# Graph network kernel: layer 1's passes in another order, degrees turned by a bf16 product of depth one, x's first loads moved up

## The chip, the cores and the metric

The kernel runs on one core of a Trainium2 chip. The metric is the device time of one launch in microseconds (us). The kernel before takes 2695.79 us (median of 3 runs, 2694.9 to 2703.81).

## The reference

Two SAGE layers, a linear layer, a residual and a layer norm, on 12,500 nodes with 256 features and 200,000 edges. The edges are sorted by `dst`, and low nodes have many more edges than high ones (`dst` is drawn as 12500 times the square of a uniform number).

```python
def sage(h, src, dst, W_l, b, W_r):
    agg = segment_sum(h[src], dst, N)              # sum over a node's edges
    deg = segment_sum(ones, dst, N)
    return (agg / maximum(deg, 1)[:, None]) @ W_l + b + h @ W_r

h = relu(sage(x, src, dst, W1_l, b1, W1_r))
h = relu(sage(h, src, dst, W2_l, b2, W2_r))
out = layernorm(x + h @ W3 + b3)
```

## The kernel before

The function `by_runs` does the work; `by_sorting` stands behind a flag for data that does not fit, and does not run here. Nodes and edges are cut into blocks and tiles of 128: 98 blocks of nodes, 1563 tiles of edges. The sums over edges are made in two ways.

**Low nodes, by counting.** The first 2,560 nodes have so many edges that a table of counts is made for them: how many edges go from each source node to each of these nodes. There are five groups (0 to 4) of 512 nodes (`COUNTED`). `count(g, to)` fills the table of group g tile by tile: DVE makes a pick and some zeros and ones (L719, L709, L725), TensorE (PE) makes two small bf16 products (L744, L746) in a bank `count_ps` of PSUM, of which there are three, and ACT casts the bank into the table (L754). The first 128 tiles, all of group 0, are added by DVE instead (L752). There are four buffers for tables; `HELD` says which group has which. A **pass** over group g (`passed`, `products`) then multiplies the whole of x by that table: for each pair of source blocks, SP loads 512 KB `rows<-x_d` (L584; three buffers, so two pairs ahead), DVE opens the packed counts (L567, L569), ACT widens them (L659, L661), and PE makes eight products of 512 columns (L682) that add up in the banks `dense_ps` and `beside_ps`. Four ACT copies (L690) end the pass.

**High nodes, by gathering.** A **round** takes four edge tiles: POOL issues four indirect DMAs of rows (`got`, L313), PE multiplies them by zeros and ones (`part_ps`, the strips, L339), ACT copies the result (L349), PE multiplies it again (`sum_ps`, L356, and L363 for the degree), and DVE adds it into a ring of sums (L369) and into a row of degrees, `degs`, which is partition 0 of the tile `spare` (L365). Layer 1 has 217 rounds.

**Blocks.** When a block's sums are complete, `first_block` finishes it in three pieces: it loads its own part x·W_r from `xw_d` (L992); it adds the bias on DVE (L1014); it turns the degrees from a row into a column, on PE by a transpose of `spare` in f32 (L1003), and DVE takes their reciprocal (L1007, L1008); `sage` multiplies the sums by W_l (L967), and h is stored. If the block's sums are known when the second piece starts, the transpose is made there, in the first third of a round, just behind the strips; the products L967 follow in the next third. Once in eight blocks, `overlap` first adds the ring's end to its beginning (DVE, L951 and L954).

**The order.** PE and POOL run in the order in which the program is written; the framework orders DVE, ACT and SP. `layer()` writes that order by a plan: it issues a round in three thirds and fills each third with pieces of dense work, until the planned load of one engine reaches a third, two thirds and all of `room_for`, which is 5.3 in layer 1. Costs such as `COST_PRODUCT` or `count_cost` are fixed numbers. When 8 rounds are left, `emptied()` writes all remaining dense work at once, and the last rounds follow without any.

Layer 1's stages (`stages_1`) are: splitting x, x·W_r and counting group 3; pass 3 with a third of the counting of groups 2, 1 and 0 (and the move of table 3 to DRAM); pass 2 with the second third; pass 1 with the rest; pass 0 with the counting of group 4; pass 4 alone. So the five passes hold 195, 190, 195, 92 and 0 counted tiles. Layer 2 makes five passes without counting.

**The start.** Edge lists and weights are loaded on SP's and ACT's queues, then DVE and PE make the tables for the first gathers, and `splitting()` loads x (`raw`, L609) and starts to multiply it.

Of the kernel before, what the change touches and what calls it, by code (L numbers as in the profile page):

```python
# [27 lines left out]
P = 128  # L28
# [23 lines left out]
def by_runs(  # L52
# [41 lines left out]
    RB = 8  # L94
# [121 lines left out]
    degs = spare[0:1]  # L216
# [167 lines left out]
    HELD = [counts[3], counts[2], counts[1], counts[0], counts[0]]  # L384
# [4 lines left out]
    near = counts_flat[1].bitcast(F32)[:, NP * CW // 2:].rearrange("p (b d) -> p b d", b=NP)[:, :, CW // 2 - NEAR:]  # L389
# [201 lines left out]

    def splitting():

        bufs = 5
        order = [*range(HOT1 // P, NB, 2), *range(0, HOT1 // P, 2)]
        assert NB % 2 == 0 and (HOT1 // P) % 2 == 0
        raw = {}

        def fetched(i):
            u = order[i]  # L600
            t = raw_pool.tile([P, 2, 2, D], F32, name="raw", bufs=bufs)
            whole = min(2, (N - u * P) // P)
            loads = []
            if whole < 2:
                left = N - (u + whole) * P
                nc.vector.memset(t[:, whole, 1], 0.0)
                loads.append(nc.sync.dma_start(t[:left, whole, 1], x[(u + whole) * P:N]))
            if whole:
                loads.append(nc.sync.dma_start(t[:, :whole, 1], x[u * P:(u + whole) * P].rearrange(  # L609
                    "(b p) d -> p b d", p=P)))  # L610
            return t

        def multiplied(i, v, x_t):
# [8 lines left out]
            b, s, pre = order[i], raw.pop(i), raw_pool.tile([P, 2, D], F32, name="pre", bufs=2)  # L622
# [10 lines left out]
        for i in range(len(order)):  # L633
            for k in range(i, min(i + bufs - 2, len(order))):
                if k not in raw:
                    raw[k] = fetched(k)
# [128 lines left out]
    def degrees(blocks):  # L765

        ps = beside_pool.tile([P, DN], F32, name="beside_ps")
        for b in range(blocks):
            n0 = b * P
            chunks = [c for c in range(HC) if at_most((c + 1) * P) + WIDEST > n0 and at_least(c * P) <= n0 + P]  # L770
            for c in chunks:
# [3 lines left out]
                for k in range(WIDEST):  # L775
                    nc.tensor.matmul(ps[:, b:b + 1], lhsT=begins[:, WIDEST - k:WIDEST - k + P],
                                     rhs=hist[:, c, k:k + 1], start=c == chunks[0] and k == 0,
                                     stop=c == chunks[-1] and k == WIDEST - 1)
# [97 lines left out]
    def stages_1(waiting):  # L876
# [13 lines left out]
        assert highs[2] - lows[2] < steps_of and highs[1] - lows[1] < steps_of  # L890
# [3 lines left out]
        yield [passed(waiting, 1, x2_d, into), (counted, cost)]  # L894
        yield [passed(waiting, 0, x2_d, into), counting(4)]
        yield [passed(waiting, 4, x2_d, into)]

    def stages_2(waiting):

        into = sums_a, sums_b  # L900
        HELD[3] = HELD[0]
# [4 lines left out]
    def all_found():  # L906

        sums_of = work.tile([P, FIELDS], F32, name="sums_of", bufs=1)
# [54 lines left out]
    def sage(b, agg, since, wl, own):  # L963

        ps = block_bank()
        for c in range(NC):
# [6 lines left out]
        given.add(b)  # L973
        nc.vector.scalar_tensor_tensor(own, ps[:, 0], rdeg[:, b:b + 1], own, op0=OP.mult, op1=OP.add)  # L974
# [14 lines left out]
    def first_block(b, agg=None):  # L989
# [7 lines left out]
        def summed(ps):  # L997
            nonlocal agg, deg_row, since
# [3 lines left out]
            r = (b % RB) * P  # L1002
            settled(nc.tensor.transpose(ps[:, NC], spare[:, r:r + P], ident), since)  # L1003

        def degree(ps):
            deg = work.tile([P, 1], F32, name="deg")
            nc.vector.tensor_scalar(deg, ps[:, NC, 0:1], 1.0, None, op0=OP.max)  # L1007
            nc.vector.reciprocal(rdeg[:, b:b + 1], deg)  # L1008

        known = of_ring and b in upto  # L1010
        if known:
            ps = turned()
# [831 lines left out]
```

## Time and profile before

| | |
|---|---|
| median of 3 runs | 2695.79 us |
| the profiled execution | 2719.84 us |
| its span, first to last instruction | 2717.6 us |
| granted PE clock, mean | 0.931 |
| split of x and x·W_r ends, pass 3 begins | about 340 us |
| end of passes 3, 2, 1, 0, 4 of layer 1 | about 546, 745, 965, 1180, 1367 us |
| layer 2's first pass begins | about 1419 us |
| layer 2's last pass ends | about 2586 us |
| HBM read, written | 541.82 MB, 93.15 MB |

The ends of the passes are the starts of the ACT copies L690. A row of the views reads: line, engine, operation, out<-in, shape, xcount, then busy time in us and the mean of one in ns, then the engine's idle time just before these instructions and what ended it. PE's products overlap one another, so that the busy time of a group is more than what the group adds to the time; the distance from one start to the next says more.

### The profile page before, as it was taken

What the parts mean: (1) busy time and instruction counts of PE and PEld (TensorE: products, weight loads), DVE (VectorE), ACT (ScalarE), POOL (GpSimd) and SP (SyncE); (2) the same over time, 40 slices, a digit from 0 to 9 for tenths busy, and PEclk for the clock granted to TensorE, in tenths of its full rate; (3) what the DMA queues carried; (4) which work ended last, traced back from release to release, by engine and by line L of the source; (5) the groups of instructions that cost most, each with busy time, mean ns of one, the idle gap of its engine ahead of it and who ended that gap; (6) DMA issues with size and microseconds to landing.
All of it is one profiled execution on the core that took longest, in us unless ns stands there. A gap on an engine that the chain in (4) does not pass through costs nothing.

```text
span 2717.6 us, 44003 instructions
## 1 busy us (share of the span) xinstructions
PE 2227.7 (82%) x13283; PEld 1535.7 (57%) x13283; DVE 1336.3 (49%) x4777; ACT 1198.1 (44%) x3325; POOL 1696.2 (62%) x1736
## 2 busy tenths in 40 slices
PE   5777788878888889878868888888888888888867
PEld 3545555555556656655635555566555655556545
DVE  5666466666667665544341233234334434444445
ACT  2434366654456655544424444443443344334312
POOL 5667566656666656666545666666666666666663
PEclk9889799999999989999978999999999999999988
DMA  8789877778787777878867877777776777667643
GB/s 225 260 267 308 283 230 230 234 231 253 253 263 238 238 240 246 267 257 272 272 196 264 273 239 232 245 233 218 245 233 208 219 230 220 197 202 226 205 138 102
DMA packets 282080, 638.07 MB, mean 235 GB/s; under 512 B 50913, under 2 KB 138795, under 8 KB 281835
## 3 DMA queue, kind: packets, MB, share of 16 engines
q1 hardware_dynamic: 193569, 407.49, 46.1%
q0 software_dynamic: 82848, 226.34, 27.1%
q8 instruction: 111, 1.82, 0.3%
q10 hardware_dynamic: 5418, 1.32, 0.3%
q14 instruction: 134, 1.10, 0.1%
HBM read 541.82 MB, written 93.15 MB: 234 GB/s over the span
## 4 chain that ended last, share of the span: by engine, by line
PE 40%; issue 6%; another core or an unknown queue 3%; DVE 2%; DMA 2%; ACT 2%; POOL 1%; SPq 0%; DVEq 0%; ACTq 0%; POOLq 0%
PE beside_ps L682 10%; PE dense_ps L682 9%; PE part_ps L339 5%; PE block_ps L967 4%; PE block_ps L1058 4%; PE sum_ps L356 3%; PE block_ps L1042 3%; PE block_ps L938 2%; POOL got L313 1%; DMA rows<-x_d 1%; ACT wide L661 1%; ACT some L349 0%; DVE sums L369 0%; DMA rows<-h_d 0%
## 5 line engine op out<-in xcount | busy, mean ns | idle before, releaser
L313 POOL DMA_INDIRECT got<-in_x_dram,src_t x863 | 871.9, 1010 | 514.1 <-issue 209.9
L313 POOL DMA_INDIRECT got<-h_d,src_t x851 | 811.3, 953 | 452.1 <-issue 225.9
L682 PE MATMUL dense_ps<-wide,rows 128*128 128x512 f32 x1960 | 885.7, 452 | 60.7 <-issue 23.6
L682 PE MATMUL beside_ps<-wide,rows 128*128 128x512 f32 x1960 | 798.0, 407 | 11.2 <-issue 7.2
L682 PEld LDWEIGHTS dense_ps<-wide,rows 128*128 128x128 f32 x1960 | 389.8, 199 | 190.0 <-issue 90.9
L661 ACT ACTIVATE wide<-spare 128x512 fp32r<-128x512 uint8 x490 | 306.7, 627 | 427.2 <-PE beside_ps L682 151.2
L682 PEld LDWEIGHTS beside_ps<-wide,rows 128*128 128x128 f32 x1960 | 388.8, 198 | 74.4 <-issue 18.6
L659 ACT CAST wide<-open 128x512 fp32r<-128x512 uint8 x490 | 300.4, 619 | 225.8 <-PE count_ps L746 72.7
L339 PE MATMUL part_ps<-got,one 128*32 128x257 f32 (+1 forms) x3472 | 299.6, 417 | 90.1 <-ACT some L349 46.5
L719 DVE TENSOR_SCALAR pick<-steps,tables,unit_t 128x175 bf16<-128x175 f16 (+3 forms) x784 | 250.5, 343 | 131.4 <-PE count_ps L746 68.8
L754 ACT CAST counts<-count_ps 128x225 f32 (+3 forms) x656 | 231.6, 353 | 160.2 <-PE count_ps L746 77.3
L369 DVE TENSOR_TENSOR sums<-sums,sum_ps 128x256 f32 x320 | 131.5, 411 | 287.1 <-PE beside_ps L682 98.5
L349 ACT COPY some<-part_ps 128x257 f32<-128x257 f32 (+1 forms) x320 | 118.1, 369 | 275.0 <-remote 67.7
L356 PEld LDWEIGHTS sum_ps<-two,some 128*128 128x128 f32 x1280 | 196.9, 200 | 46.9 <-issue 16.1
L356 PE MATMUL sum_ps<-two,some 128*128 128x128 f32 x1280 | 209.9, 287 | 16.2 <-issue 10.0
L263 DVE TENSOR_TENSOR one<-lo_t,lane_b 128x128 f32<-128x128 bf16 x430 | 122.6, 285 | 180.5 <-PE beside_ps L682 42.6
L339 PEld LDWEIGHTS part_ps<-got,one 128*32 128x32 f32 x3472 | 71.3, 111 | 240.9 <-issue 142.1
L746 PE MATMUL count_ps<-pick,low 128*128 128x175 bf16 (+3 forms) x784 | 176.6, 254 | 30.7 <-issue 15.3
L744 PE MATMUL count_ps<-aft,low 128*128 128x25 bf16 x652 | 117.3, 194 | 57.4 <-ACT counts L754 25.9
L618 PE MATMUL dense_ps<-w1r_sb,own_t 128*128 128x256 f32 x392 | 119.8, 433 | 46.2 <-issue 21.7
L746 PEld LDWEIGHTS <-low 128*128 128x128 bf16 x784 | 89.0, 120 | 99.0 <-issue 82.7
L974 DVE SCALAR_TENSOR_TENSOR own<-block_ps,rdeg,own 128x256 f32<-128x256 f32 x196 | 93.8, 478 | 98.5 <-PE sum_ps L356 17.0
(231 smaller groups left out, 2674.6 us busy)
## 6 DMA issues: line engine op xcount, KB each, us to landing
rows<-x_d SPq DMA_DIRECT2D x245, 512.0 KB
rows<-h_d SPq DMA_DIRECT2D x245, 512.0 KB
x_d<-raw SPq DMA_DIRECT2D x49, 512.0 KB
h_d<-split SPq DMA_DIRECT2D x98, 256.0 KB
got<-in_x_dram,src_t POOLq DMA_INDIRECT x863
got<-h_d,src_t POOLq DMA_INDIRECT x851
xw_d<-pre SPq DMA_DIRECT2D x49, 256.0 KB
own<-xw_d SPq DMA_DIRECT2D x98, 128.0 KB
```

The costliest lines, as they stand in the source:

```text
L263: nc.vector.tensor_tensor(one, lo[:, a:a + n * (G - 1) + 1:n].unsqueeze(2).to_broadcast([P, G, W]), lane_b[:, :W].unsqueeze(1).to_broadcas ...
L313: rows = nc.gpsimd.indirect_dma_start(out=g[:, j, X0:], out_offset=None, in_=table, in_offset=bass.IndirectOffsetOnAxis(ap=index[:, e:e + ...
L339: strip = nc.tensor.matmul(part_ps[j * W:(j + 1) * W, :width], lhsT=one[:, j], rhs=g[:, row, DW - width:], start=r == 0, stop=r == n - 1)
L356: nc.tensor.matmul(sum_ps[:, c], lhsT=some[:, x0 + c * P:x0 + (c + 1) * P], rhs=two, start=True, stop=True)
L369: adds.append(nc.vector.tensor_add(own, own, sum_ps[:, :NC]).ins)
L618: nc.tensor.matmul(ps[:, v * D:(v + 1) * D], lhsT=x_t[:, c], rhs=w1r_sb[:, c], start=c == 0, stop=c == NC - 1)
L659: nc.scalar.copy(wide.bitcast(F32R), counted)
L661: nc.scalar.activation(wide.bitcast(F32R), counted, AF.Copy, accum_out=seen[:, b % FIELDS, b // FIELDS:b // FIELDS + 1])
L682: nc.tensor.matmul(ps[c], lhsT=own, rhs=wide[u].bitcast(F32R), start=u + k == 0, stop=u == NB - 1 and k == 1)
L719: nc.vector.tensor_scalar(r[:, :w * NP], steps[:, :w * NP], key_t[g][:, t - lo_g:t - lo_g + 1], unit_t[:, t:t + 1], op0=OP.is_equal, op1=O ...
L746: nc.tensor.matmul(ps[:, :w * NP], lhsT=s, rhs=r[:, :w * NP], start=j == 0 and alone, stop=j == n_in - 1, skip_group_check=not alone)
L754: copies.append(nc.scalar.copy(to[:, :, bass.ds(off_act.at(t), w)], of).ins)
```

## The change

1. The passes of layer 1 run in the order 3, 2, 1, 4, 0. The counting of groups 2, 1, 4 and 0 is cut into four equal parts, one beside each of the passes 3, 2, 1 and 4; pass 0 runs alone at the end. The five passes now hold 169, 169, 157, 175 and 0 counted tiles. The buffers for the tables change places (`HELD`, `near`), and `room_for` goes from 5.3 to 5.2.
2. `degs` holds bf16. The transpose is replaced by a product of depth one: the row of 128 degrees is the weights, a single 1.0 the moving operand, and the column lands in the second half of the bank that `sage` already uses. It stands in `sage`, right ahead of the products with W_l, whether the block's sums are known earlier or not. A test that a degree is under 255.5 joins the tests on the data, and those are now added up in `all_found()` at the end of layer 2.
3. `degrees()` makes 221 products of one column instead of 260.
4. `w1r` and the first three loads of x are written ahead of the small loads and of the second copy of `dst` (`nxt_i`).

```diff
-    degs = spare[0:1]
+    degs = spare.bitcast(BF16)[0:1, :RN + P]
...
-    HELD = [counts[3], counts[2], counts[1], counts[0], counts[0]]
+    HELD = [counts[0], counts[2], counts[1], counts[0], counts[3]]
...
-                for k in range(WIDEST):
+                n_k = max(ROOMS[c * P // 32:(c + 1) * P // 32])
+                for k in range(n_k):
...
-        counted = chain(*(count(g, HELD[g]) for g in (2, 1, 0)))
-        cost = sum(counting(g)[1] for g in (2, 1, 0)) / 3
-        steps_of = sum(highs[g] - lows[g] for g in (2, 1, 0)) // 3
+        later_groups = 2, 1, 4, 0
+        counted = chain(*(count(g, HELD[g]) for g in later_groups))
+        cost = sum(counting(g)[1] for g in later_groups) / 4
+        tiles = [highs[g] - lows[g] for g in later_groups]
+        steps_of = sum(tiles) // 4
...
-        yield [passed(waiting, 1, x2_d, into), (counted, cost)]
-        yield [passed(waiting, 0, x2_d, into), counting(4)]
-        yield [passed(waiting, 4, x2_d, into)]
+        yield [passed(waiting, 1, x2_d, into), (islice(counted, steps_of), cost)]
+        yield [passed(waiting, 4, x2_d, into), (counted, cost)]
+        yield [passed(waiting, 0, x2_d, into)]
...
-    def sage(b, agg, since, wl, own):
+    def sage(b, agg, since, wl, own, deg_row=None):
         ps = block_bank()
+        if deg_row is not None:
+            product = nc.tensor.matmul(ps[:, 1, 0:1], lhsT=deg_row, rhs=lane_b[0:1, 1:2], start=True, stop=True)
+            settled(product, since)
...
+        if deg_row is not None:
+            deg = work.tile([P, 1], F32, name="deg")
+            nc.vector.tensor_scalar(deg, ps[:, 1, 0:1], 1.0, None, op0=OP.max)
+            nc.vector.reciprocal(rdeg[:, b:b + 1], deg)
...
-            settled(nc.tensor.transpose(ps[:, NC], spare[:, r:r + P], ident), since)
...
-        known = of_ring and b in upto
-        if known:
-            ps = turned()
-            summed(ps)
         nc.vector.tensor_add(own, own, biases[:, 0])
         yield 0.22, 0.4, 0.0
-        if of_ring and not known:
-            ps = turned()
-            summed(ps)
         if of_ring:
-            degree(ps)
-        h = sage(b, agg, since, w1l_sb, own)
+            overlap(b, True)
+            agg, deg_row = ring(b)
+            since = upto[b]
+        h = sage(b, agg, since, w1l_sb, own, deg_row)
...
+    w1r_sb = weight(w1r, "w1r_sb", "wr", nc.sync)
+    for i in range(3):
+        raw[i] = fetched(i)
...
-    nc.scalar.copy(spare, zero.to_broadcast([P, RN + P]))
+    nc.scalar.copy(degs, zero[0:1].to_broadcast([1, RN + P]))
...
-        layer(gathers_1, first_block, 3, staged(stages_1), 5.3, 8)
+        layer(gathers_1, first_block, 3, staged(stages_1), 5.2, 8)
```

The numbers of instructions hardly change. On PE, 78 transposes become 78 products of one column, and 39 of the products in `degrees()` go. All else is moved.

The first place is PE's order in one round of layer 1, from the strips (L339) of a round to a block's products with W_l; `dense_ps` and `beside_ps` are a pass's products. Before:

```order
L339 MATMUL part_ps<-got_99,one 32x257 x4
L1003 MATMUL block_ps<-ident,spare 128x128
L682 MATMUL dense_ps<-wide,rows 128x512
L682 MATMUL beside_ps<-wide,rows 128x512
L682 MATMUL dense_ps<-wide,rows 128x512
L682 MATMUL beside_ps<-wide,rows 128x512
L967 MATMUL block_ps<-w1l_sb,sums 128x256 x2
```

And after, from the strips of another such round:

```order
L339 MATMUL part_ps<-got_98,one 32x257 x4
L680 MATMUL dense_ps<-wide,rows 128x512
L680 MATMUL beside_ps<-wide,rows 128x512
L680 MATMUL dense_ps<-wide,rows 128x512
L680 MATMUL beside_ps<-wide,rows 128x512
L974 LDWEIGHTS spare
L974 MATMUL block_ps<-lane_b,spare 128x1
L977 MATMUL block_ps<-w1l_sb,sums 128x256 x2
```

The turn of the degrees has moved from behind the strips to the products with W_l; four products of the pass now lie ahead of it.

The second place is SP's queue at the end of layer 1's last pass: `rows<-x_d` are the pass's loads, `own` a block's part, `h_d` the stores of finished blocks. Before:

```order
L584 DMA rows<-x_d 128x1024 x3
L1027 DMA h_d<-own 128x256
L1030 DMA h_d<-split 128x512
L584 DMA rows<-x_d 128x1024
L992 DMA own<-xw_d 128x256
L584 DMA rows<-x_d 128x1024 x2
L1027 DMA h_d<-own 128x256
L1030 DMA h_d<-split 128x512
L584 DMA rows<-x_d 128x1024
L992 DMA own<-xw_d 128x256
```

And after:

```order
L584 DMA rows<-x_d 128x1024 x2
L1023 DMA h_d<-own 128x256
L1026 DMA h_d<-split 128x512
L584 DMA rows<-x_d 128x1024 x3
L1006 DMA own<-xw_d 128x256
L584 DMA rows<-x_d 128x1024 x7
```

With the smaller `room_for`, less of the last pass fits between the rounds, and the rest is written in one piece: 104 products of the pass follow one another on PE without anything between (before 32), and SP's last ten loads of rows have one other DMA among them.

The third place is SP's queue at the start, from its last load of a piece of `dst`; `counts1_120<-in_dst_dram` is `nxt_i`. Before:

```order
L1115 DMA counts0_119<-in_dst_dram 1x64
L1102 DMA counts1_120<-in_dst_dram 128x12x128
L1111 DMA counts1_120<-in_dst_dram 26x128
L1115 DMA counts1_120<-in_dst_dram 1x63
L1155 DMA w1r_sb_160<-in_L0_gnn_W1_r_dram 128x2x256
L609 DMA raw_254<-in_x_dram 128x2x256
L609 DMA raw_256<-in_x_dram 128x2x256
```

And after:

```order
L1111 DMA counts0_119<-in_dst_dram 1x64
L1126 DMA w1r_sb_146<-in_L0_gnn_W1_r_dram 128x2x256
L606 DMA raw_148<-in_x_dram 128x2x256
L606 DMA raw_150<-in_x_dram 128x2x256
L606 DMA raw_152<-in_x_dram 128x2x256
L1098 DMA counts1_120<-in_dst_dram 128x12x128
```

W1_r and three loads of x have passed the 768 KB of `nxt_i`.

More of the change, by code (lines that the diff above doesn't have):

```diff
@@ L590, in by_runs, with fetched @@
     AHEAD_OF = set()
-    def splitting():
[L594 to L611, printed above, removed]
+    X_BUFS = 5
+    x_order = [*range(HOT1 // P, NB, 2), *range(0, HOT1 // P, 2)]
+    assert NB % 2 == 0 and (HOT1 // P) % 2 == 0
+    raw = {}
+    def fetched(i):
+        u = x_order[i]
+        t = raw_pool.tile([P, 2, 2, D], F32, name="raw", bufs=X_BUFS)
+        whole = min(2, (N - u * P) // P)
+        if whole < 2:
+            left = N - (u + whole) * P
+            nc.vector.memset(t[:, whole, 1], 0.0)
+            nc.sync.dma_start(t[:left, whole, 1], x[(u + whole) * P:N])
+        if whole:
+            nc.sync.dma_start(t[:, :whole, 1], x[u * P:(u + whole) * P].rearrange("(b p) d -> p b d", p=P))
+        return t
+    def splitting():
         def multiplied(i, v, x_t):
@@ L621, in multiplied @@
                 return COST_AHEAD
-            b, s, pre = order[i], raw.pop(i), raw_pool.tile([P, 2, D], F32, name="pre", bufs=2)
+            b, s, pre = x_order[i], raw.pop(i), raw_pool.tile([P, 2, D], F32, name="pre", bufs=2)
             nc.scalar.copy(pre, ps.rearrange("p (b d) -> p b d", b=2))
@@ L632, in splitting @@
         ps, last = None, None
-        for i in range(len(order)):
-            for k in range(i, min(i + bufs - 2, len(order))):
+        for i in range(len(x_order)):
+            for k in range(i, min(i + X_BUFS - 2, len(x_order))):
                 if k not in raw:
@@ L906, in all_found @@
     def all_found():
+        many = work.tile([P, NB], F32, name="many", tag="x_sb")
+        nc.vector.tensor_scalar(many[:, HOT1 // P:], rdeg[:, HOT1 // P:], 1.0 / 255.5, 0.0, op0=OP.is_le, op1=OP.add,
+                                accum_out=test())
+        bad_ps = block_bank()
+        nc.tensor.matmul(bad_ps[0:1, 0, :TESTS], lhsT=ones, rhs=bad, start=True, stop=True)
+        n_unfit = work.tile([1, 1], F32, name="n_unfit", bufs=1)
+        nc.vector.tensor_reduce(n_unfit, bad_ps[0:1, 0, :TESTS], axis=mybir.AxisListType.X, op=OP.add)
         sums_of = work.tile([P, FIELDS], F32, name="sums_of", bufs=1)
@@ L995, in first_block @@
         yield 0.0, 0.0, 0.0
-        def summed(ps):
-            nonlocal agg, deg_row, since
+        nc.vector.tensor_add(own, own, biases[:, 0])
+        yield 0.22, 0.4, 0.0
+        if of_ring:
             overlap(b, True)
@@ L1147, in by_runs @@
             "(g j l) -> j g l", j=G, l=2 * P)[:, :, 0])
+    nxt_i = edges(dst, 1, later_on, "nxt_i", FAR, nc.sync)
+    last_edges(nxt_i, dst, 1)
+    with nc.allow_non_contiguous_dma(reason="one edge of each tile"):
         nc.scalar.dma_start(f1_i, dst[None, 0:HC * P * P:P])
         nc.scalar.dma_start(fours_i, dst[0:P * P:P * G][:, None, None].to_broadcast([P // G, G, 1]))
-    loads = []
-    def weight(w, name, tag, queue=nc.scalar):
-        t = consts.tile([P, NC, w.shape[1]], F32, name=name, tag=tag)
-        loads.append(queue.dma_start(t, w.rearrange("(c p) f -> p c f", p=P)))
-        return t
-    w1r_sb, w1l_sb = weight(w1r, "w1r_sb", "wr", nc.sync), weight(w1l, "w1l_sb", "wl")
+    w1l_sb = weight(w1l, "w1l_sb", "wl")
     biases = consts.tile([P, 2, D], F32, name="biases")
```

26 lines of the change are left out of this document (8 added, 18 removed).

## The prediction, made before the changed kernel ran

> **What bounds the kernel now.** I read the page's busy times first, then the busy time of each engine by stage, then the idle time just before groups of instructions.
>
> ```profile
> span 2717.6 us, 44003 instructions
> PE 2227.7 (82%) x13283; PEld 1535.7 (57%) x13283; DVE 1336.3 (49%) x4777; ACT 1198.1 (44%) x3325; POOL 1696.2 (62%) x1736
> ```
>
> PE is the busiest by far. The next view has one row for each pass of layer 1 (order 3, 2, 1, 0, 4): length, busy time of PE, PEld, DVE, ACT and POOL, granted clock, DMA share and GB/s.
>
> ```profile
> 340.00:546.00 206.00, 173.78 (x1184) 114.68 (x1183) 130.69 (x542) 129.41 (x344) 130.00 (x130) 0.96 0.74 230
> 546.00:745.00 199.00, 171.57 (x1048) 112.89 (x1047) 130.87 (x516) 98.94 (x233) 123.49 (x122) 0.95 0.78 246
> 745.00:965.00 220.00, 189.96 (x1322) 132.75 (x1321) 151.38 (x625) 130.94 (x375) 144.97 (x143) 0.98 0.78 246
> 965.00:1180.00 215.00, 181.86 (x1122) 124.74 (x1121) 123.00 (x469) 116.12 (x291) 137.35 (x140) 0.93 0.79 253
> 1180.00:1367.00 187.00, 159.10 (x849) 111.94 (x849) 74.64 (x262) 83.89 (x179) 106.93 (x112) 0.93 0.80 262
> ```
>
> PE idles 32, 27, 30, 33 and 28 us in the five passes: 14 to 16% in each, whether DVE is busy for 151 us of 220 or for 75 of 187. So PE's work and the small waits between its pieces set the time, and time is won by less PE work or fewer PE waits. Layer 2's passes take the rest, from 1419 us on; its PE order is the same row for row, so I count it at nothing.
>
> **Part 1: the degrees' turn.** L1003 is the transpose, L776 a bf16 product of one column, the nearest thing to the new product.
>
> ```profile
> L1003 PE MATMUL block_ps<-ident,spare 128*128 128x128 f32 x78 | 26.4, 339 | 18.6 <-DVE spare L954 11.5 <-issue 4.0 <-DVE sums L369 3.2
> L776 PE MATMUL beside_ps<-hist,begins 128*128 128x1 bf16 x260 | 10.1, 166 | 8.4 <-DVE begins L773 6.8 <-issue 1.1 <-DVE sums L369 0.4
> L776 PEld LDWEIGHTS <-begins 128*128 128x128 bf16 x260 | 9.4, 103 | 12.0 <-DVE begins L773 8.1 <-issue 1.6 <-DVE open L567 0.8
> L967 PEld LDWEIGHTS block_ps<-w1l_sb,sums 128*128 128x128 f32 x392 | 75.8, 200 | 21.5 <-issue 8.0 <-DVE open L567 0.5 <-DVE deg L1007 0.4
> 1333.03 0.33 PE L1003 MATMUL block_ps<-ident,spare 128*128 128x128 f32 x1
> 1333.12 0.48 PE L682 MATMUL dense_ps<-wide,rows 128*128 128x512 f32 x1
> ```
>
> A transpose lasts 339 ns but keeps the next product back by 0.09 us only (1333.03 to 1333.12). A product of one column adds 10.1/260 = 0.04 us. So at least 78 × (0.09 − 0.04) = 4 us go; by the means, 78 × (0.339 − 0.166) = 13.5 us. The other end: the new product is too short to cover the load of the sums behind it, and if those 200 ns stood open each time, it would cost 78 × (0.20 + 0.04 − 0.09) = 12 us more than before. 260 loads of weights of 103 ns were busy for 9.4 us together, so such loads run beside one another, and I stay with a gain. The row is nearer to 4 than to 13.5: I take **7 us less**.
>
> [...]
>
> Then the 18.6 us that PE waits ahead of the turn. The longest wait:
>
> ```profile
> 1219.76 0.61 PE L356 MATMUL sum_ps<-two,some 128*128 128x128 f32 x4
> 1227.86 0.47 PE L1003 MATMUL block_ps<-ident,spare 128*128 128x128 f32 x1 [5.89 <-DVE spare L954]
> 1226.40 0.28 DVE L365 TENSOR_TENSOR spare<-spare,sum_ps 1x128 f32 x1 [2.35 <-remote]
> 1227.53 0.27 DVE L954 TENSOR_TENSOR spare<-spare 1x128 f32<-1x128 f32 x1
> 1227.80:1233.00 5.20, 5.14 (x13) 4.11 (x14) 1.80 (x8) 2.17 (x6) 2.84 (x3) 0.50 0.64 217
> ```
>
> The turn is put down to DVE's L954. But DVE began L365, which needs products that PE shows at 1219.76, only at 1226.40, and it was free before: something else held everybody. Such a wait goes to whatever stands there next. So I leave the 11.5 us of L954 as they are. The other 7.1 (`issue` and `sums L369`) come from the turn standing right behind the strips; the new product stands four products of the pass later. I take **5 us less**, between 0 and 18.6.
>
> After that wait PE ran at a granted clock of 0.50 for 5 us. [...]
>
> DVE's maximum and reciprocal now wait for the new product, but L974 behind them waits for the products with W_l anyway. ACT's and DVE's operations on the degrees keep their counts and lengths (1x128). All this I cost at nothing.
>
> **Part 2: counting over four passes.** One row for each group and pass: pass 3; pass 2 (two rows); pass 1 (two); pass 0 (three).
>
> ```profile
> L744 PE MATMUL count_ps<-aft,low 128*128 128x25 bf16 x195 | 35.1, 195 | 31.3 <-ACT counts L754 17.1 <-PE count_ps L746 5.7 <-ACT some L349 4.0
> ...
> L746 PE MATMUL count_ps<-pick,low 128*128 128x175 bf16 (+2 forms) x191 | 37.8, 245 | 18.5 <-issue 11.4 <-DVE pick L719 4.3 <-DVE counts L752 1.1
> L744 PE MATMUL count_ps<-aft,low 128*128 128x25 bf16 x72 | 12.2, 193 | 10.0 <-issue 5.6 <-ACT counts L754 4.2
> ...
> L746 PE MATMUL count_ps<-pick,low 128*128 128x125 bf16 (+1 forms) x198 | 38.5, 228 | 10.1 <-DVE pick L719 5.8 <-issue 2.7 <-DVE low L709 1.1
> L744 PE MATMUL count_ps<-aft,low 128*128 128x25 bf16 x190 | 32.1, 193 | 18.8 <-ACT counts L754 8.1 <-issue 6.8 <-ACT some L349 2.9
> ...
> L682 PE MATMUL dense_ps<-wide,rows 128*128 128x512 f32 x196 | 90.1, 459 | 15.1 <-DMA rows<-x_d 8.3 <-issue 3.8 <-ACT wide L659 2.9
> L746 PE MATMUL count_ps<-pick,low 128*128 128x250 bf16 (+1 forms) x99 | 27.9, 282 | 1.2 <-issue 1.1
> L744 PE MATMUL count_ps<-aft,low 128*128 128x25 bf16 x97 | 19.1, 197 | 0.8 <-issue 0.4 <-DVE aft L725 0.2
> ```
>
> PE waits 31.3, 28.5 and 28.9 us for counting where a pass holds about 195 tiles, and 2.0 us where it holds 99: 90.7 in all. After, the passes hold 169, 169, 157 and 175. A straight line through 99 tiles, 2.0 us, and 195 tiles, 29.6 us, gives 22 + 22 + 19 + 24 = 87: 4 us less. If the wait grows with the square above 99, it is 17 + 17 + 12 + 19 = 65: 26 less. If every tile waits as in the three full passes (29.6/195 = 0.15 us), it is 670 × 0.15 = 100: 10 more. The four rows lie on the line by its making and say nothing of a curve, so I take **4 us less**, with −26 and +10 as ends. Pass 0 is the warning: it hardly waits for counting, yet idles as much as the others, because its products wait for rows instead.
>
> **Part 3: the run at the end.** With `room_for` 5.2, 104 products of the last pass stand together, where 32 did. Those 32:
>
> ```profile
> 1354.22 0.48 PE L682 MATMUL dense_ps<-wide,rows 128*128 128x512 f32 x1
> 1356.16 0.47 PE L682 MATMUL dense_ps<-wide,rows 128*128 128x512 f32 x1
> ...
> 1362.95 0.51 PE L682 MATMUL dense_ps<-wide,rows 128*128 128x512 f32 x1 [2.45 <-DMA rows<-x_d]
> 1366.38 0.75 PE L339 MATMUL part_ps<-got,one 128*32 128x257 f32 x8
> 1357.09 0.32 SPq L1030 DMA_DIRECT2D h_d<-split  x1
> 1357.51 0.43 SPq L584 DMA_DIRECT2D rows<-x_d  x1
> ```
>
> Eight products, one pair of blocks, take 1.94 us undisturbed (1354.22 to 1356.16). The four pairs took 12.2 us, 3.04 each, since the last load left SP only at 1357.51, behind a store. The 72 products more are nine pairs: 17.5 us of work, or 20.5 at pass 4's busy share (159.10/187). At 1.94 us a pair the run saves 3 us, at 3.04 it costs 7. SP's new order has ten loads with one other DMA among them, so I take 2.5 us a pair: **2 us more**.
>
> **Part 4: the start and the rest.**
>
> ```profile
> 26.55 0.73 PE L1253 MATMUL after<-counts 1*128 1x160 f32 x2
> 28.43 0.69 PE L938 MATMUL block_ps<-ident,raw 128*128 128x128 f32 x2 [1.15 <-DMA raw<-in_x_dram]
> 23.85 0.90 SPq L609 DMA_DIRECT2D raw<-in_x_dram  x2
> 28.23 1.15 ACT L1262 COPY spare<-zero 128x1152 f32<-128x1152 f32 x1
> 29.28 0.38 ACT L940 ACTIVATE own_t<-block_ps 128x256 f32<-128x256 f32 x1
> ```
>
> x's first load left SP at 23.85 us and PE waited 1.15 us for it. Now it leaves some 12 us sooner. But the transposes stand behind L1253 on PE, and ACT can copy them only when it has cleared its tiles at 29.28: that cover hides the gain. I take 0; 1.2 us at most, and as much lost if the small loads on ACT's queue come later beside x. The 39 products fewer in `degrees()` are 39/260 of 18.5 us (10.1 busy, 8.4 idle), 2.8 us, in a stage where DMA is busier than PE: **1 us less**. The new test at the end of layer 2 stands beside other work: nothing.
>
> **Sum**: −7 − 5 − 4 + 2 − 1 = −15 us on the profiled execution: 2719.84 − 15 = 2705. That execution took 24 us more than the median of the runs; the waits in question are the same in both, so I take the 15 us from the median: 2695.79 − 15 = **2681**.
>
> **The rivals.** (A) My forecast, 2681, own range 2671 to 2687. (B) The counting waits fall with the square: 22 us more won, 2659. For it: 99 tiles wait for almost nothing. Against: the idle share of passes 0 and 4. (C) The waits move on: what counting and the turn no longer cost is lost to rows and `issue`, as in pass 0; only the work goes, −7 − 1 + 2 = −6, 2690. For it: 14 to 16% of idling everywhere. (D) On the other side: the run at the end starves. If only one load of rows is under way at a time, a pair takes 5.44 us (1357.51 to 1362.95), and thirteen pairs cost 13 × (5.44 − 2.5) = 38 us more: 2681 + 38 = 2719. It ends slower than before by 0.3% from 4.3 us a pair on. For it: the wait of 2.45 us above, and the slow clock behind such waits. Against: three buffers, no gathers beside it once POOL's four buffers are full, and SP's order.
>
> **How the numbers follow.** 0.3%, about what a measurement of this kernel can tell from no change, is 8 us: below 2688 is faster. Chances: A 0.42, B 0.19, C 0.25, D 0.14. Faster is A and B, 0.61; the same is C, 0.25; slower is D, 0.14. The range takes in B with some of the ends of part 1 (the 18.6 us of waits) and most of D: 2650 to 2714.
>
> **What would show it.** The new product with its idle time in place of L1003's 26.4 and 18.6: right if the idle time ahead of it is near 13 us. The idle time ahead of the two counting groups in the four passes: 87 us by A, 65 by B. If those fall while each pass still idles 14 to 16%, C is right. The last ten loads of rows and the products beside them: right at 2 to 3 us a pair, wrong from 4.3 on. PE's first transpose of x: no earlier than 27.3 us. The forecast is wrong if the passes together, 340 to 1367 us before, are not shorter by 10 to 20 us, or if layer 2, whose order did not change, moves by more than a few us.

## The result, and the profile after

The changed kernel takes 2721.29 us (median of 14 runs, 2708.91 to 2735.66), the kernel before 2702.08 us (14 runs, 2694.40 to 2716.78) on the same chip: a ratio of 1.0065, 95% interval 1.0045 to 1.0086. It is 19 us slower, where the prediction said 2681 us, 15 us faster. The profiled execution took 2729.83 us.

The page of the changed kernel begins so (span; then busy time, share and count for each engine):

```profile
span 2727.6 us, 43881 instructions
PE 2232.3 (82%) x13244; PEld 1532.2 (56%) x13244; DVE 1333.2 (49%) x4779; ACT 1190.1 (44%) x3325; POOL 1688.7 (62%) x1736
```

PE has 39 products fewer and is busy 4.6 us longer. By pass of layer 1 (order now 3, 2, 1, 4, 0; columns as in the prediction):

```profile
349.00:553.00 204.00, 176.51 (x1150) 114.52 (x1150) 122.65 (x509) 121.64 (x322) 126.61 (x129) 0.94 0.72 232
553.00:761.00 208.00, 175.16 (x1163) 115.53 (x1161) 129.03 (x524) 125.37 (x335) 135.13 (x138) 0.98 0.78 253
761.00:977.00 216.00, 185.56 (x1108) 126.07 (x1109) 138.64 (x530) 95.59 (x215) 133.32 (x135) 0.93 0.75 242
977.00:1200.00 223.00, 191.59 (x1311) 133.86 (x1311) 151.40 (x621) 128.20 (x372) 143.73 (x146) 0.97 0.77 248
1200.00:1381.00 181.00, 153.81 (x797) 105.00 (x795) 68.74 (x243) 81.83 (x177) 94.29 (x98) 0.93 0.78 259
```

The five passes take 1032 us, before 1030 (336 to 1366). They begin at 349 us instead of 336. Layer 2 hardly moved: from the first product of its first pass to the end 1296.2 us, before 1298.9. So in these two traces, whose spans differ by 10 us, 12 us went in the stage ahead of the passes, and nothing came back in them. The groups that the prediction priced (busy, mean ns, idle before):

```profile
L974 PE MATMUL block_ps<-lane_b,spare 1*128 1x1 bf16 x78 | 13.5, 173 | 2.5 <-DVE spare L961 1.9 <-issue 0.5
L977 PE MATMUL block_ps<-w1l_sb,sums 128*128 128x256 f32 x392 | 115.7, 420 | 4.1 <-issue 4.0
L744 PE MATMUL count_ps<-pick,low 128*128 128x175 bf16 (+3 forms) x784 | 175.4, 254 | 35.8 <-DVE pick L717 18.5 <-issue 11.2 <-DVE split L552 1.7
L742 PE MATMUL count_ps<-aft,low 128*128 128x25 bf16 x652 | 117.8, 195 | 81.4 <-issue 32.1 <-ACT counts L752 29.6 <-ACT some L349 6.9
```

The same groups before (the transpose itself, L1003, stands in the prediction):

```profile
L967 PE MATMUL block_ps<-w1l_sb,sums 128*128 128x256 f32 x392 | 109.1, 402 | 7.9 <-issue 7.6 <-DVE deg L1007 0.3
L746 PE MATMUL count_ps<-pick,low 128*128 128x175 bf16 (+3 forms) x784 | 176.6, 254 | 30.7 <-issue 15.3 <-DVE pick L719 11.0 <-DVE low L709 1.3
L744 PE MATMUL count_ps<-aft,low 128*128 128x25 bf16 x652 | 117.3, 194 | 57.4 <-ACT counts L754 25.9 <-issue 15.3 <-ACT some L349 6.9
```

In this trace the turn's own group fell from 26.4 busy and 18.6 idle to 13.5 and 2.5, more than I took. Yet the products with W_l behind it (now L977) grew from 402 to 420 ns on average, and the idle time ahead of counting rose from 88 us to 117.

### The profile page after: what moved, and what is told of

Read it like the earlier page. It is cut to its first block, busy times and chain, and to the rows that moved or that the text cites. A ratio compares the mean times of both kernels' runs of the same rounds, so it can differ in the third digit from the quotient of the medians.

```text
span 2727.6 us, 43881 instructions
## 1 busy us (share of the span) xinstructions
PE 2232.3 (82%) x13244; PEld 1532.2 (56%) x13244; DVE 1333.2 (49%) x4779; ACT 1190.1 (44%) x3325; POOL 1688.7 (62%) x1736
## 4 chain that ended last, share of the span: by engine, by line
PE 74%; issue 8%; DVE 4%; another core or an unknown queue 4%; DMA 3%; ACT 3%; POOL 1%; ACTq 0%; SPq 0%; DVEq 0%; POOLq 0%
PE dense_ps L680 17%; PE beside_ps L680 17%; PE part_ps L339 9%; PE block_ps L977 7%; PE sum_ps L356 5%; PE count_ps L744 4%; PE block_ps L1054 4%; PE block_ps L1038 3%; PE dense_ps L616 3%; PE block_ps L945 3%; PE count_ps L742 2%; DMA rows<-x_d 1%; POOL got L313 1%; ACT wide L659 1%
## 5 line engine op out<-in xcount | busy, mean ns | idle before, releaser
L339 PE MATMUL part_ps<-got,one 128*32 128x257 f32 (+1 forms) x3472 | 295.2, 413 | 85.5 <-ACT some L349 44.7
L744 PE MATMUL count_ps<-pick,low 128*128 128x175 bf16 (+3 forms) x784 | 175.4, 254 | 35.8 <-DVE pick L717 18.5
L339 PEld LDWEIGHTS part_ps<-got,one 128*32 128x32 f32 x3472 | 70.7, 111 | 230.9 <-issue 128.4
L744 PEld LDWEIGHTS <-low 128*128 128x128 bf16 x784 | 90.0, 120 | 125.1 <-issue 109.5
L947 ACT ACTIVATE own_t<-block_ps 128x256 f32<-128x256 f32 x196 | 75.6, 386 | 129.6 <-PE block_ps L945 37.8
```

The costliest lines, as they stand in the source:

```text
L339: strip = nc.tensor.matmul(part_ps[j * W:(j + 1) * W, :width], lhsT=one[:, j], rhs=g[:, row, DW - width:], start=r == 0, stop=r == n - 1)
L744: nc.tensor.matmul(ps[:, :w * NP], lhsT=s, rhs=r[:, :w * NP], start=j == 0 and alone, stop=j == n_in - 1, skip_group_check=not alone)
```

## The experiments

One thing has to be known to read them: the chips of these runs fall into two kinds. On some the kernel before takes 2702 to 2740 us, on others 2316 to 2319. The view of PE's waits tells them apart (us in total, times, longest); its two longest rows are shown for each kind. The changed kernel on a slower chip (run `after_2`):

```profile
PE count_ps L742 <- issue: 32.5, 38, 2.2
PE dense_ps L616 <- issue: 26.7, 18, 6.7
```

The changed kernel on a faster chip (`r_after`):

```profile
PE part_ps L339 <- DMA got<-h_d,src_t: 64.5, 68, 3.2
PE part_ps L339 <- DMA got<-in_x_dram,src_t: 34.9, 26, 3.6
```

On the slower kind PE waits 147 to 180 us for `issue`, that is for nothing that the profile shows (172 in the trace of before, 159 in that of the change), and its granted clock is about 0.93; on the faster kind it waits 0 to 6 us for `issue` and the clock is 0.97 to 0.98. What `issue` stands for there no run can show. The prediction was for the slower kind. Each ratio below is to the kernel before on the same chip; the half width of its interval is 0.1 to 0.3%. Each kernel has one trace; the runs of each section below are of one chip, and the only trace of the kernel before is of the first.

### One part undone (faster kind; before 2315.52 us)

Each kernel is the changed one with one part as before: `u_turn` with the transposes, `u_count` with the old order and counting, `u_x` with the old loads, and `u_room` with the old `room_for`:

```diff
-        layer(gathers_1, first_block, 3, staged(stages_1), 5.2, 8)
+        layer(gathers_1, first_block, 3, staged(stages_1), 5.3, 8)
```

> The changed kernel with the old turn of the degrees (78 f32 transposes in a bank of their own, maximum and reciprocal ahead of the products with W_l); all else as changed. Compared with the kernel before; the changed kernel stood at 1.0065 (+17.5 us). Theory 1 (the turn's place costs it: in sage the same bank of the pool of two stays held until DVE has done maximum, reciprocal and the product's sum, as in the stall of 14.54 us at 175.65 us): ratio 0.996 to 1.001, and the stall at 160 to 175 us is gone. Theory 2 (the run of 104 products at the end costs it): 1.005 to 1.008. Theory 3 (the counting over four passes costs it): 1.005 to 1.008. Theory 4 (x's early loads cost it, the start being overtaken by 22 rounds): 1.005 to 1.008.

> The changed kernel with the old order of passes (3, 2, 1, 0, 4) and counting in three of them; all else as changed, room_for 5.2 too. Theory 1 (the turn's place): 1.004 to 1.008. Theory 2 (the run at the end, which here is set by the same room): 1.004 to 1.008, unless the old order shortens the run. Theory 3 (counting; PE's idle time ahead of the two counting groups rose from 88.1 to 117.2 us instead of falling by 4): 0.995 to 0.999, and that idle time back near 88 us. Theory 4: 1.005 to 1.008.

> The changed kernel with x's first loads where they were, behind the small ones; all else as changed. Theory 4 (the early loads disturb the start: rounds 0 to 16 came some 2 us sooner, and all of it and more was lost by round 22): 0.997 to 1.002, with pass 3 beginning near 336 us and not near 349. Theories 1, 2 and 3: 1.005 to 1.008, pass 3 beginning near 349 us.

> The changed kernel with room_for 5.3 as before; all else as changed, so the run of products of the last pass at layer 1's end is short. Theory 2 (the run costs it: rounds 200 to 210 took 87.6 us instead of 70.8): 0.998 to 1.002, with rounds 200 to 210 back near 71 us. Theories 1, 3 and 4: 1.004 to 1.008.

Measured: 0.9996 without the new turn, 1.0091 without the new counting, 0.9995 without the early loads, 1.0027 with room 5.3. The counting helps, against theory 3. The others can't be read without the whole on the same kind of chip, which comes next.

### The whole, and one part alone (faster kind; before 2319.20 us)

> The changed kernel once more, unchanged, since the first four runs fell on a chip where the kernel before takes 2315 us and not 2702. Theory 5 (the parts add up: the four kernels with one part undone stood at -0.04, +0.91, -0.05 and +0.27%; if each is the whole less its part, the whole is their sum over three, +0.36%, with turn +0.40, counting -0.55, early x +0.41, room +0.09): ratio 1.002 to 1.005. Theory 6 (the loss belongs to the long waits of all engines on the first chip, which this one does not have): 0.998 to 1.001. Theory 7 (the loss is in the kernel's order and goes with any part undone): 1.005 to 1.008.

> The kernel before with the new turn of the degrees alone (bf16 product of depth one in sage's bank, degrees as bf16). Theory 1 (the turn's place costs it) and theory 5: 1.002 to 1.006, with more idle time of PE ahead of the products that need the next bank of the pool of two. The prediction's part 1 (12 us less): 0.993 to 0.997. If the parts do not add up (theory 7): 0.998 to 1.002.

> The kernel before with the new order of passes and counting over four passes alone; room_for 5.3. Theory 5: 0.992 to 0.997. The prediction's part 2 (4 us less, ends -26 and +10): 0.989 to 1.004, likeliest 0.998. Theory 3 (counting costs): 1.003 to 1.008.

> The kernel before with x's first loads ahead of small ones alone. Theory 4 (the early loads disturb the start) and theory 5: 1.002 to 1.006, with rounds 20 to 40 some 1 to 4 us later than without. The prediction's part 4 (hidden at the start): 0.999 to 1.001.

Measured: the whole 1.0018 (1.0000 to 1.0035), the turn alone 1.0062 (1.0038 to 1.0085), the counting alone 0.9938 (0.9919 to 0.9957), the early loads alone 0.9996. On this kind a gain of 14 us and a loss of 14 us stand against each other. The turn goes the wrong way, and the early loads don't show. Against the whole, the kernels with one part undone now read: turn +0.2%, counting −0.7%, early loads +0.2%, room −0.1%; only the counting's is clear of the intervals. And the parts don't add up: `u_turn`, which has the counting, the early loads, the shorter `degrees()` and room 5.2, stands at 0.9996 where the counting alone stands at 0.9938. Some 13 us of the counting's gain are lost in what stands beside it, and no run of this kind says in which part.

What the turn takes on PE, its timeline shows in steps from start to start (start, length). The kernel with early loads alone, whose turn is the old one:

```profile
795.78 0.64 PE L339 MATMUL part_ps<-got,one 128*32 128x257 f32 x8
796.35 0.33 PE L1001 MATMUL block_ps<-ident,spare 128*128 128x128 f32 x1
796.52 0.19 PE L742 MATMUL count_ps<-aft,low 128*128 128x25 bf16 x1
796.55 0.22 PE L744 MATMUL count_ps<-pick,low 128*128 128x125 bf16 x1
```

The kernel with the new turn alone:

```profile
802.31 0.39 PE L682 MATMUL dense_ps<-wide,rows 128*128 128x512 f32 x1
802.54 0.39 PE L682 MATMUL beside_ps<-wide,rows 128*128 128x512 f32 x1
802.86 0.17 PE L974 MATMUL block_ps<-lane_b,spare 1*128 1x1 bf16 x1
802.96 1.13 PE L977 MATMUL block_ps<-w1l_sb,sums 128*128 128x256 f32 x4
```

The transpose kept the next product back by 0.17 us (796.35 to 796.52), 0.085 where a product of the pass followed: some 10 us over 78. The new product has 0.32 us ahead of it where a pass's product is followed by the next in 0.23 (802.31 to 802.54), 0.10 behind it, and the second product with W_l starts 0.32 us after the first instead of 0.215 (medians of the 78). Together 0.30 × 78 = 24 us: 14 more than before, as much as the run lost. Whether that is the cause, the next runs test. The loads of weights in the same kernel:

```profile
L776 PEld LDWEIGHTS <-begins 128*128 128x128 bf16 x260 | 9.1, 100 | 5.7 <-DVE begins L773 4.0 <-issue 0.7 <-DVE pick L719 0.4
L974 PEld LDWEIGHTS <-spare 1*128 1x128 bf16 x78 | 7.1, 91 | 34.4 <-issue 20.2 <-DVE spare L961 9.6 <-DVE sums L369 1.4
```

In this trace a load of one row takes 91 ns, one of 128 rows 100: 127 rows fewer save 9 ns.

The early loads, in DVE's timeline of the kernel with them alone:

```profile
27.48 0.35 DVE L1240 CAST counts<-counts 4x391 f32<-4x391 int32 x1 [7.12 <-DMA counts<-in_dst_dram]
```

The same cast in the kernel with counting alone, where the loads stand as before:

```profile
22.27 0.35 DVE L1237 CAST counts<-counts 4x391 f32<-4x391 int32 x1 [1.94 <-DMA counts<-in_dst_dram]
```

With x's loads ahead, DVE waits 5.2 us longer for the small loads, everything behind that cast on DVE comes later, and PE's first transpose of x starts at 31.06 us instead of 28.03. In the time of the run that is not seen.

### The turn's place and its form (faster kind; before 2318.00 us)

`p_op` puts the new product where the transpose stood, `p_place` the transpose where the new product stands, and `t_full` gives the new product weights of 128 rows:

```diff
 p_op
-            settled(nc.tensor.transpose(ps[:, NC], spare[:, r:r + P], ident), since)
+            settled(nc.tensor.matmul(ps[:, NC, 0:1], lhsT=deg_row, rhs=lane_b[0:1, 1:2], start=True, stop=True), since)
 p_place, against the new turn
-            product = nc.tensor.matmul(ps[:, 1, 0:1], lhsT=deg_row, rhs=lane_b[0:1, 1:2], start=True, stop=True)
+            product = nc.tensor.transpose(ps[:, 1, 0:P], spare[:, r:r + P], ident)
 t_full, against the new turn
-            product = nc.tensor.matmul(ps[:, 1, 0:1], lhsT=deg_row, rhs=lane_b[0:1, 1:2], start=True, stop=True)
+            product = nc.tensor.matmul(ps[:, 1, 0:1], lhsT=degs_all[:, r:r + P], rhs=row_0, start=True, stop=True)
```

`best_full` is t_full's turn with the new counting and the shorter products in `degrees()`.

> The kernel before with the new product (bf16, depth one, degrees as bf16) at the old place: right behind the strips, in a bank of its own, maximum and reciprocal ahead of the products with W_l. Theory 1 (the place in sage costs it: the bank of the pool of two is held over maximum and reciprocal): 0.997 to 1.000. Theory 8 (a product whose weights fill only part of the array, 1*128 or 128*32, has its load stand open, and so has the product behind it; with the new turn alone PE took 0.329 us to the new product instead of 0.233 to the product with W_l, 0.102 on to that, and 0.320 instead of 0.215 to the next, together 0.303 x 78 = 24 us, where the old transposes behind the strips took 0.085 to 0.165, some 10 us): here the strips, 128*32, have paid for the switch already, so 0.998 to 1.002. Theory 9 (the product itself costs it wherever it stands): 1.004 to 1.007.

> The kernel before with the old f32 transpose at the new place, in sage's bank ahead of the products with W_l, maximum and reciprocal behind those. Theory 1 (the place costs it): 1.004 to 1.007. Theory 8 (weights of 128*128 here, so no load stands open for the switch; by products of that form some 0.11 us each, 78 x 0.11 = 9 us, as much as the old turn): 0.998 to 1.001, with 0.23 us to the transpose and 0.215 between the first two products with W_l. Theory 9: 0.998 to 1.001.

> The kernel before with the new turn alone, but with weights of all 128 rows (the degrees' row with the rows beneath it, against a column that is 1 in row 0 and 0 elsewhere), so that the form is 128*128; place, type and one column as in the changed kernel. Theory 8: 0.998 to 1.001, with 0.238 us from the pass's product to this one and 0.215 to 0.231 between the first two products with W_l. Theory 1 and theory 9: 1.004 to 1.007, as with the new turn alone (1.0062).

> The kernel before with the counting over four passes and the new order of passes, the shorter products in degrees(), and the turn with weights of all 128 rows; room_for 5.3, x's loads where they were. Theory 8: 0.991 to 0.996, as the counting alone (0.9938) or a little less. Theory 1 and theory 9 (the turn still costs its 0.6%): 0.998 to 1.002.

Measured: 1.0006, 1.0033 (1.0012 to 1.0054), 1.0040 (1.0023 to 1.0057), 0.9982 (0.9968 to 0.9996). Theory 9 is out: behind the strips the same product costs nothing that the interval of `p_op` (0.9989 to 1.0023) would show. Theory 8 is right on the steps of PE and wrong on the time. In t_full's timeline the product with weights of 128 rows follows as closely as another of the pass would:

```profile
804.23 0.39 PE L684 MATMUL dense_ps<-wide,rows 128*128 128x512 f32 x1
804.46 0.39 PE L684 MATMUL beside_ps<-wide,rows 128*128 128x512 f32 x1
804.69 0.18 PE L977 MATMUL block_ps<-row,spare 128*128 128x1 bf16 x1
804.73 0.89 PE L980 MATMUL block_ps<-w1l_sb,sums 128*128 128x256 f32 x3
```

0.23 us to the product and 0.04 behind it, though the second product with W_l is still late (0.30 instead of 0.215). But the whole gain by the steps, 0.18 × 78 = 14 us, did not come: 1.0062 fell to 1.0040 only, 5 us, and the two intervals overlap. And the old transpose at the new place, which by its steps costs no more than at the old, lost 0.33%. So theory 8 missed on `p_place` and `t_full` (0.998 to 1.001 expected), and theory 1 is nearer on both: the place costs by itself, by these two runs 8 to 9 us, give or take 4 to 5. `best_full` says the same a third time: 0.9982 where the counting alone stood at 0.9938, 10 us more, in theory 1's range and not in theory 8's. The 14 us by steps and the 8 to 9 of the place together are more than the 14 that the turn lost; so the price of the one-row form in time is not shown. Part of the place's cost is in the idle time ahead of the turn, here in the lines of `p_op`:

```profile
L1002 PE MATMUL block_ps<-lane_b,spare 1*128 1x1 bf16 x78 | 13.5, 173 | 9.0 <-DVE spare L954 8.6 <-DVE own L974 0.4
```

And in those of `p_place`:

```profile
L968 PE MATMUL block_ps<-ident,spare 128*128 128x128 f32 x78 | 22.2, 285 | 18.4 <-DVE spare L954 10.4 <-DVE own L982 4.9 <-DVE sums L369 3.1
```

In sage, the turn waits for the bank that the last block's sum (`own`) still holds: 4.9 us against 0.4. The rest I did not find in a single wait.

### On a chip of the slower kind (before 2739.24 us)

`count_short` is the kernel before with the new counting, order and shorter `degrees()`; `count_room` adds `room_for` 5.2.

> The changed kernel, unchanged, for the chip. Additive theory (from the eleven kernels so far: turn's place +8.6 us, its form of one row +3, counting -12.8, early x +4.4, room 5.2 and the shorter products +2.8, together +6): on a chip where the kernel before takes about 2318 us and PE's waits for issue come to 1 to 3 us: 1.001 to 1.004. On a chip like the first one (2702 us, 172 us of PE's waits put down to issue): 1.0045 to 1.0086 again.

> The new turn of the degrees alone, once more (1.0062 from six runs). On a chip of 2318 us: 1.004 to 1.008 if the first figure holds, 1.002 to 1.004 if only its place costs. On a chip like the first: if the turn makes the whole loss there 1.007 to 1.012, if counting or the early loads make it 1.003 to 1.006.

> The kernel before with the new order of passes, counting over four of them and the shorter products in degrees(), nothing else; room_for 5.3. If counting's gain is its own (0.9938 alone): 0.992 to 0.996. If that was an accident of the one program: 0.998 to 1.001. On a chip like the first, where PE's idle time ahead of counting rose from 88 to 117 us: 0.992 to 0.996 if the gain is from shorter passes of counting, 1.000 to 1.004 if it is lost to waits there.

> The same with room_for 5.2, so that 104 products stand together at layer 1's end. The prediction's part 3 (2 us more; rival D: 38 us more when only one load is under way): ratio to the kernel with 5.3 of 1.001 by part 3, 1.016 by rival D; if the room changes how rounds and counting mesh and takes the gain back (the kernel with everything but the turn stood at 0.9996 although counting alone stood at 0.9938): 0.998 to 1.001 against the kernel before.

Measured: the whole 1.0034 (1.0008 to 1.0060), the turn alone 0.9998 (0.9974 to 1.0023), the counting 0.9937 (0.9912 to 0.9961), with room 5.2 1.0004 (0.9978 to 1.0031). The counting wins 0.6% on both kinds. The turn costs nothing here that 7 us of noise would show, though its steps are the same (0.33, 0.10 and 0.32 us in `turn_2`); why, no run shows. And room 5.2 takes away the whole gain of the counting, 2720.66 to 2742.22 us.

What the counting won, in the lines of PE from the first pass of layer 1 to the first of layer 2. Before:

```profile
L682 PE MATMUL dense_ps<-wide,rows 128*128 128x512 f32 x981 | 446.4, 455 | 39.7 <-DMA rows<-x_d 15.6 <-ACT sums L690 10.3 <-issue 9.0
...
L744 PE MATMUL count_ps<-aft,low 128*128 128x25 bf16 x553 | 98.2, 194 | 57.3 <-ACT counts L754 25.9 <-issue 15.3 <-ACT some L349 6.9
```

`count_short`:

```profile
L682 PE MATMUL dense_ps<-wide,rows 128*128 128x512 f32 x980 | 442.3, 451 | 18.4 <-ACT wide L659 6.8 <-issue 6.6 <-DMA rows<-x_d 3.2
...
L744 PE MATMUL count_ps<-aft,low 128*128 128x25 bf16 x553 | 97.5, 194 | 78.0 <-ACT counts L754 31.6 <-issue 24.4 <-ACT some L349 7.2
```

The waits ahead of counting rose by 21 us, and those ahead of the passes' own products fell by 21, most of it waiting for rows. That cancels. (Before is a trace of the first chip; `turn_2`, of the same chip as `count_short` and without its counting, has 60.3 us ahead of L744's products and 40.0 ahead of the passes'.) What is left is 6 us before the first pass and PE's busy time between these ends, 911.8 to 898.7 us. The rows of these stretches (length, then PE, PEld, DVE, ACT, POOL, clock, DMA share, GB/s), before and `count_short`:

```profile
336.00:1419.00 1083.00, 911.84 (x5722) 617.89 (x5719) 641.36 (x2524) 577.35 (x1472) 667.94 (x672) 0.94 0.77 245
330.00:1403.00 1073.00, 898.65 (x5719) 614.26 (x5717) 637.01 (x2523) 566.99 (x1472) 670.08 (x672) 0.95 0.76 247
```

PE makes all but the same number of products in both, and the granted clock is 0.95 instead of 0.94. In the trace of before the passes' products start 0.43 us apart where the clock is 0.50 (1228.4 to 1229.9 us) and 0.23 where it is 1.00 (1358.4 to 1360.2). If all busy time goes with the clock like that, the clock alone makes 911.8 × 0.94/0.95 = 902 us of it, an estimate. By that estimate 10 of the 13 us come with the higher clock; whether the counting brought that, no run shows. On the faster kind, where the traces of `only_x` and `only_count` are of one chip and the clock is 0.97 in both, the same stretch is 12 us shorter, of which 3 is busy time and 9 idle time: ahead of counting (26.9 to 21.1 us) and ahead of the passes' products (19.2 to 13.3).

### Room and early loads alone (slower kind; before 2740.04 us)

> The kernel before with room_for 5.2 alone. The prediction's part 3 (2 us more, at the end of layer 1 alone): 1.000 to 1.001. Rival D: 1.014. Theory 10 (the room shifts rounds through all of layer 1, more of them beside the first passes, and that costs what count_room lost on count_short, 0.67%): 1.005 to 1.008. Theory 11 (that loss is in the meshing of this room with the new counting): 0.997 to 1.001.

> x's first loads ahead of small ones alone, once more. On a chip of about 2318 us: 0.9985 to 1.002, as before (0.9996). On a chip like the first: if the early loads make the rest of the loss there (the changed kernel 1.0034 and 1.0065, counting 0.9937, room 5.2 0.67%, the turn 0.9998), 1.003 to 1.006; if they don't, 0.998 to 1.002. On either, PE's first transpose of x some 3 us later than without, behind DVE's wait for the small loads.

Measured: room 5.2 alone 1.0043 (1.0025 to 1.0062), the early loads alone 1.0003 (0.9979 to 1.0027). The room costs 12 us by itself (7 to 17 by the interval), 18 to 22 with the new counting. What it changes, the products of the strips tell (L339, eight to a round), by pass: length, then busy and count of PE and PEld, clock, DMA share, GB/s. Before (the trace of the first chip):

```profile
336.00:547.00 211.00, 21.34 (x260) 5.08 (x256) 0.95 0.73 227
547.00:745.00 198.00, 21.65 (x248) 5.12 (x248) 0.95 0.78 246
745.00:971.00 226.00, 23.08 (x288) 5.70 (x288) 0.97 0.78 248
971.00:1180.00 209.00, 22.28 (x272) 5.44 (x272) 0.94 0.78 252
1180.00:1366.00 186.00, 18.39 (x224) 4.45 (x224) 0.93 0.80 263
```

With room 5.2 alone:

```profile
344.00:560.00 216.00, 22.09 (x272) 5.40 (x272) 0.96 0.69 223
560.00:758.00 198.00, 21.18 (x256) 5.14 (x256) 0.97 0.78 255
758.00:1000.00 242.00, 23.88 (x296) 5.85 (x296) 0.94 0.72 231
1000.00:1216.00 216.00, 22.98 (x280) 5.60 (x280) 0.95 0.77 251
1216.00:1385.00 169.00, 15.72 (x192) 3.82 (x192) 0.96 0.80 265
```

Room 5.2 moves four to five rounds out of the last pass into the four before it. Those grow by 28 us (5, 0, 16 and 7), the last shrinks by 17, and 8 more are lost ahead of the first pass. These two traces are of two chips. `count_short` and `count_room` are of one, and there the four passes grow by 26 us (8, 6, 9 and 3), the last shrinks by 14, and 14 are lost ahead of the first pass (330 to 344 us). Beside `early_x_2`, which has room 5.3 on the chip of `only_room`, the five passes are only 6 us longer. So where the rounds go is certain; how the 12 us divide over the stages is not. On the faster kind the room cost nothing beside the new turn (1.0027 with 5.3, 1.0018 with 5.2).

The stage ahead of the passes, in which the changed kernel lost its 12 us, ends late in two sorts of kernel on the slower kind: at 346 to 349 us in the three traces with early loads, at 344 in the two others with room 5.2, and at 330 to 341 in the three with neither. `early_x_2` lost nothing in the end that 7 us of noise would show, so this does not say which of the two costs the time.

The best version measured is the kernel before with the new counting and order alone: 0.9938 on the faster kind and, with the shorter products in `degrees()`, 0.9937 on the slower. On each it is faster than both kernels.

## Why the prediction was wrong

Two terms of the sum failed, the room and the turn, and a part of the loss stays open.

**Part 3, the run at the end: the first step that failed.** The prediction said of `room_for` 5.2 that "104 products of the last pass stand together, where 32 did", took 2.5 us a pair, and made of it "2 us more". The run came out as said. In the trace of the change:

```profile
1347.97 0.47 PE L680 MATMUL dense_ps<-wide,rows 128*128 128x512 f32 x1 [0.21 <-DMA rows<-x_d]
...
1380.66 0.39 PE L680 MATMUL beside_ps<-wide,rows 128*128 128x512 f32 x1
```

103 steps in 32.7 us, 2.54 us a pair of blocks. But the room doesn't act at the end alone: it moves rounds through all of layer 1, and I priced only the place to which the eye went. Alone it costs 12 us, with the new counting 18 to 22. Rival D had the sign and not the mechanism: over these products PE waited 3.2 us for rows in all. That its 2719 us lies next to the measured 2721 is luck.

**Part 1, the turn: the second step that failed.** Twelve us less were forecast, 7 of PE work and 5 of waits; measured were 14 us more on the faster kind and 0 ± 7 on the slower. Of the "7 us less" nothing is there: by the steps it is 14 us more, just beyond the end of +12 that the prediction had put down as the case where the loads stand open. The failed inference was from 260 loads in a row, which run beside one another (103 ns each, 9.4 us busy together), to a load of one row between products of 128 rows. The "5 us less" of waits did show in the first trace of the change (18.6 to 2.5 us), but it is no property of the new turn: in `after_2` the group waits 8.0 us and in `turn_2`, with the turn alone, 15.1. "DVE's maximum and reciprocal … I cost at nothing": the new place, where they stand behind the product, costs 8 to 9 us on the faster kind.

**Part 2, the counting.** Right in sign, mis-sized: "4 us less" was 17 (14 on the faster kind), within the ends of −26 and +10. On the slower kind the mechanism was another: the waits that I drew a line through rose by 22 us, waits for rows fell by as much, and the gain lay in PE's busy time, with a higher clock, and ahead of the passes. On the faster kind those waits did fall, by 6 us. The test of A against B (87 or 65 us) decided nothing, at 117. The base of 90.7 us was wrong too: one wait of 3.5 us at 545.9 us stands in the rows of both the first and the second pass, and 0.9 us of L746 in the first was left out; it is 88.1.

**Part 4.** Right: nothing at the end, and PE's first transpose "no earlier than 27.3 us". It came at 31.29, behind the small loads; that loss was named, at 1.2 us, and is 2.9. The 1 us for `degrees()` was not run by itself. **Layer 2** moved by less than 3 us: right. **Rival C**, waits that move on while each pass still idles 14 to 16%, describes the passes (13 to 16%), though not its 6 us of gain.

**The sum.** By single parts on the slower kind: turn 0, counting −17, room +12 to +18, early loads +1, together −4 to +2. The whole measured +9 on one such chip and +18 on the first. Those 7 to 22 us stay open. On the chip of `after_2` they are within the noise, since each ratio there is good to 7 us only; on the first chip no part was run. All parts but the turn and the early loads stood at 1.0004, so what is left would lie in what these two do beside the others, and that pair was not run on this kind. The first trace of the change has one long wait ahead of the passes, for a bank that DVE's L988 frees (PE's timeline):

```profile
175.65 0.69 PE L945 MATMUL block_ps<-ident,raw 128*128 128x128 f32 x2 [14.54 <-DVE own L988]
```

That alone is not it: the second trace (`after_2`) reaches the first pass at 345.9 us, only 3 us sooner, and from 40 us to there PE has no wait above 6.7 us.

## What to carry to other kernels

A number that sets a planner's order changes the order everywhere: compare rows over the whole stage before pricing the one place where the change shows most. A wait in a group is not a price: look at it in a second trace, and price an edit by the steps from start to start around it, with what stood there and what will. Even the steps are not the time (in `t_full` 14 us fewer by steps were 5 us in time), so run the new form and the new place apart. By its steps here, the product with one row of weights did better behind the strips (one place of `p_op`: 0.58 us from the first strip to it, where the transpose of `only_x` has 0.57, and 0.10 to the next product, where that has 0.17) than between products of 128 rows (`only_turn`: 0.32 to it, where a pass's product has 0.23).

## What was not expected of the hardware

- From a product of 128x512 of a pass to the one-row product it is 0.32 to 0.33 us from start to start in `only_turn` and in the trace of the change, and to the strips (128*32) as much; to another product of form 128*128 it is 0.23. From the last strip to the next product it is 0.31, in the traces of before and of the change. The step behind the one-row product is 0.10 us, behind the same product with 128 rows (`t_full`) 0.04. What PE does in these steps, no run shows.
- Behind the one-row product (`only_turn` and the change) the second f32 product with W_l starts 0.32 us after the first, behind the short product with 128 rows of weights (`t_full`) 0.30; right behind a product of a pass it is 0.215.
- The same program takes 2721 and 2750 us on two chips and 2323 on another (the changed kernel), at a granted clock of 0.93 and 0.98, with PE idle 495 and 509 us in the one and 232 in the other; and the parts of one change weigh differently on them (the turn alone +0.6% and 0).
